# First layer of a graph network: count products taken in pairs between dense steps

## Chip, core and metric

The kernel runs on one core of a Trainium2 chip. The metric is the device time of one execution in microseconds (us). The core has five engines that matter here: TensorE (PE in the profile, and PEld for its weight loads), VectorE (DVE), ScalarE (ACT), GpSimd (POOL), which issues the gathers, and SyncE (SP), which issues plain transfers.

## What is computed

A graph of 6,250 nodes and 100,000 edges, sorted by destination, goes through a layer norm and four layers. Each layer adds up every node's neighbours and passes the sum through three dense stages.

```
def agg(h):
    return jax.ops.segment_sum(h[src], dst, num_segments=N)     # N = 6250
for l in range(3):
    h = x + agg(x)
    h = relu(h @ W1s[l] + b1s[l])
    h = relu(h @ W2s[l] + b2s[l])
    x = h @ W3s[l] + b3s[l]
h = x + agg(x)
...                                   # a last layer of the same form, 256 -> 256 -> 64 -> 256
out = x0 + h                          # x0: the kernel's input; the layers get relu(layernorm(x0))
```

## The kernel before

**Blocks.** The nodes lie in 49 blocks of 128. A part of the destination blocks is summed by gathers: POOL fetches one row per edge (line 1622, `rows<-table,idxN`) and DVE adds them up (line 1658, `sums<-sums,rows`). All other destination blocks, 30 of them in the first layer, are summed by matrix products with a matrix of counts: how many edges lead from node s to node d. The counts are built once, in the first layer, kept in DRAM as bytes (`mat`), and read again in the later layers.

**A dense step.** In `product` (from line 1914) the destination blocks are taken in panels of three or four, and each panel goes over the 49 source blocks. One source block of one panel is a dense step: ACT turns the byte counts into a right operand `a` (line 1908), and PE makes four products with it (line 1937, `agg<-a,XY`: two halves of the channels, each with a rounded value and a remainder), 512 columns wide, or 384 in a panel of three. `a` is made three steps ahead (`AHEAD = 3`), in a ring of five buffers.

**A step that builds counts.** In `build` (from line 1229) one step makes the counts of 16 destination nodes against all source nodes, an eighth of a destination block, with one-hot operands. DVE writes `lo`, 128 x 512 (line 1200, one comparison), for every step, and `hi`, 128 x 784 (line 1200, a comparison and a multiplication), once for two steps. PE then makes four count products with them (line 1254, `bp<-hi,lo`, 98 columns, bf16), and ACT, or DVE in every eighth step, moves the result out of `bp` (lines 1262 and 1264). `lo`, `hi` and the PSUM tile `bp` have two buffers each. The program writes the `lo` of step k+1 at step k, so DVE can be up to two steps ahead of PE, and must wait for the products of step k-1 before it writes `lo` of step k+1. The `hi` of steps k+2 and k+3 follows it.

**Side work.** The generator `listed` (from line 1706) is called once per dense step in the first layer. In seven of its steps DVE prepares short tiles (lines 1817 to 1828, `moved`), PE turns them (line 1835, `bp<-ident,moved`, with a `bp` buffer of the same two), and DVE reads the result into `clT` (lines 1845 to 1847). Below, "the listing" means those seven.

**Order.** All engines' instructions are written out by hand in the order of the Python code, and each engine runs its own in that order. In the first layer the order inside one dense step u is: side work that is due (adds of gathered rows, dense stages of an earlier panel), one step of `listed`, the next `a`, then as many building steps as a table `goals` asks for, then the four products of step u:

```
                prepare(u + 1 + (AHEAD if l == 0 else AHEAD + 2))
                if beside is not None:
                    goal = goals[u - PRE]
                    while built[0] < goal:
                        next(beside)
                        built[0] += 1
```

`goals` is a list with one entry per dense step: the number of building steps that must be done by then. It rises in a straight line over each panel, so that the counts of the next panel are there in time: 28 of 257 are done before the first dense step, and then 28 more in 32 dense steps of the first panel, later 32 in 49, fewer at the end. POOL's gathers are issued by a virtual clock that each product advances by a planned cost (`passed`), and each gather waits for the product that was last written before it.

Of the kernel before, what the change touches and what calls it, by code (L numbers as in the profile page):

```python
# [420 lines left out]
def sorted_edges(  # L421
# [46 lines left out]
    NT = -(-N // P)  # L468
# [628 lines left out]
    with tc.manual_schedule():  # L1097
# [760 lines left out]
        last = [len(panels[l]) - 1 for l in range(NLAYER + 1)]  # L1858
# [99 lines left out]
        def yields(slots):  # L1958
            return UNITS * slots + (slots > TOP)

        total = yields(BUILT)
        built, goals = [0], []
        u0, g0 = 0, UNITS * FIRST + EARLY
        for p in range(last[0] + 1):
# [2 lines left out]
            goals.extend(g0 + (g1 - g0) * (u - u0) // (u1 - u0) for u in range(u0 + 1, u1 + 1))  # L1967
            u0, g0 = u1, g1
        assert g0 == total
        goals = goals + [total] * (NT * (last[0] + 1) - u0)  # L1970
        late = None
        chunks = ctx.enter_context(tc.tile_pool(name="chunks", bufs=1))
        with tc.tile_pool(name="hots", bufs=1) as hots, tc.tile_pool(
# [41 lines left out]
def kernel(  # L2015
# [27 lines left out]
    rest = (x, src, dst, W1s, b1s, W2s, b2s, W3s, b3s, cW1, cb1, cW2, cb2, cW3, cb3, out)  # L2043
    earlier = []
    sorted_edges(tc, good, earlier, *rest)
    done = nc.values_load(good[0:1, 0:1], min_val=0, max_val=1)
    with tc.If(done == 0):
# [27 lines left out]
```

## Time and profile before

| | us |
|---|---|
| median of 3 runs | 2008.25 |
| lowest, highest | 2006.13, 2008.99 |
| profiled execution, its own time | 2005.61 |
| span of its profile | 2003.8 |
| first and last count product | 135.8, 667.4 |
| first dense step | 173.6 |

The profile is of one execution. Its lines give, for a group of equal instructions, the line of the code, the engine, the operation, the tiles written and read (`out<-in`), the count, the busy time, the mean time of one, and the idle time of the engine before them with what ended it. In a timeline each row has the start, the time until the last instruction of the row ends, and in brackets how long the engine had been idle. A PE instruction's time is longer than its share of the pipeline: what matters there is from start to start.

### The profile page before, as it was taken

To read this page: it belongs to the slowest core of one execution; us is meant where nothing else is said; L and a number is where in the kernel's file an instruction comes from. 1 tells how busy PE (TensorE), PEld (TensorE's weight loads), DVE (VectorE), ACT (ScalarE), POOL (GpSimd) and SP (SyncE) were. 2 spreads that over 40 slices of the span, in tenths; PEclk is the share of its full clock that TensorE was granted. 3 is DMA by queue.
4 is the path that set the end of the run, shared out by engine and by line. 5 is a ranking of instruction groups with operands and counts; after the bars stand their busy time and mean duration, and the time that the engine had idled before them with its cause. 6 is when DMAs were issued, how large, how long until landed. Compare 5 with 4: busy or idle time off the path is not lost.

```text
span 2003.8 us, 29049 instructions
## 1 busy us (share of the span) xinstructions
PE 1885.4 (94%) x9236; PEld 1472.8 (74%) x9236; DVE 1034.1 (52%) x2213; ACT 1077.4 (54%) x2164; POOL 1311.1 (65%) x1444
## 2 busy tenths in 40 slices
PE   5955999999999899999999999999999999999997
PEld 3734766777777787777789777777788877777775
DVE  7877887677756343333344353333345354343433
ACT  4734776776766564444445464444445564455442
POOL 2526666766766556777777466676777466777775
PEclk9876999999999999999999999999999999999999
DMA  5523656665656475555656575564657576565553
GB/s 167 176 74 115 201 176 197 203 210 183 206 187 212 155 241 163 173 182 162 185 169 206 168 248 168 159 198 149 187 168 230 160 216 202 184 200 171 180 176 106
DMA packets 252333, 361.40 MB, mean 180 GB/s; under 512 B 33352, under 2 KB 206312, under 8 KB 252154
## 3 DMA queue, kind: packets, MB, share of 16 engines
q1 hardware_dynamic: 188160, 190.34, 30.0%
q0 software_dynamic: 61952, 166.87, 27.5%
q10 hardware_dynamic: 2058, 2.25, 0.4%
q8 instruction: 74, 1.21, 0.3%
q14 instruction: 89, 0.73, 0.1%
HBM read 292.33 MB, written 67.40 MB: 180 GB/s over the span
## 4 chain that ended last, share of the span: by engine, by line
PE 83%; DVE 6%; DMA 4%; issue 2%; POOL 2%; ACT 1%; SPq 0%; DVEq 0%; ACTq 0%; POOLq 0%
PE agg L1937 66%; PE ps L1514 6%; PE ps L1417 6%; DMA rows<-table,idxN 2%; PE bp L1254 2%; POOL rows L1622 1%; DVE hi L1200 1%; PE pt L1685 1%; PE bp L1046 1%; DVE lo L1200 1%; POOL lane L1743 1%; PE ps L1431 1%; DMA wd<-joined,starts 0%; DVE ws L768 0%; DMA lane<-padded,at 0%
## 5 line engine op out<-in xcount | busy, mean ns | idle before, releaser
L1937 PE MATMUL agg<-a,XY 128*128 128x512 f32 (+1 forms) x6272 | 1513.1, 393 | 15.4 <-DVE a L1910 6.9
L1622 POOL DMA_INDIRECT rows<-table,idxN x1121 | 1087.1, 970 | 473.9 <-PE agg L1937 211.0
L1937 PEld LDWEIGHTS agg<-a,XY 128*128 128x128 f32 x6272 | 1146.7, 189 | 249.2 <-issue 12.7
L1908 ACT CAST a<-at 128x512 fp32r<-128x512 uint8 (+1 forms) x1249 | 709.4, 602 | 237.9 <-PE agg L1937 226.8
L1658 DVE TENSOR_TENSOR sums<-sums,rows 128x512 f32<-128x512 f32 x477 | 332.1, 696 | 499.6 <-DMA rows<-table,idxN 444.8
L1910 DVE CAST a<-at 128x512 fp32r<-128x512 uint8 (+1 forms) x312 | 141.7, 460 | 171.4 <-PE agg L1937 147.8
L1262 ACT CAST at<-bp 128x392 uint16<-128x392 f32 x227 | 110.3, 489 | 128.0 <-PE bp L1254 122.2
L1417 PE MATMUL ps<-h,w 128*128 128x512 f32 (+2 forms) x336 | 135.3, 546 | 0.0
L1514 PE MATMUL ps<-w,h 128*128 128x256 f32 x588 | 133.7, 379 | 0.0
L1200 DVE TENSOR_TENSOR lo<-lanes,pairs 128x512 bf16<-128x512 bf16 x256 | 107.1, 424 | 45.1 <-PE bp L1254 44.3
L1254 PEld LDWEIGHTS <-lo 128*128 128x128 bf16 x1028 | 57.5, 103 | 96.8 <-DVE lo L1200 41.9
L1254 PE MATMUL bp<-hi,lo 128*128 128x98 bf16 x1028 | 95.2, 219 | 33.4 <-DVE lo L1200 27.1
L1514 PEld LDWEIGHTS ps<-w,h 128*128 128x128 f32 x588 | 111.2, 190 | 15.9
L596 POOL DMA_INDIRECT table<-zz,ids x72 | 72.9, 1013 | 66.3 <-DVE zz L1519 48.1
L1654 ACT COPY sums<-rows 128x512 f32<-128x512 f32 x74 | 43.8, 593 | 122.5 <-DMA rows<-table,idxN 101.1
L1420 ACT ACTIVATE h<-ps,bias 128x512 f32<-128x512 f32 (+2 forms) x84 | 51.7, 636 | 95.1 <-PE ps L1417 95.1
L1417 PEld LDWEIGHTS ps<-h,w 128*128 128x128 f32 x336 | 63.0, 193 | 52.6 <-issue 37.8
L1519 DVE TENSOR_TENSOR zz<-ps,w 128x512 f32<-128x512 f32 (+1 forms) x81 | 50.5, 639 | 96.0 <-PE ps L1514 89.3
L1693 ACT ACTIVATE h<-pt,bias 128x256 f32<-128x256 f32 (+1 forms) x84 | 33.1, 446 | 124.3 <-PE pt L1685 124.2
L1344 DVE TENSOR_TENSOR XY<-back,XY 128x256 fp32r<-128x256 f32 x138 | 55.1, 423 | 46.9 <-ACT XY L1343 46.0
L1951 ACT ACTIVATE h<-agg,bias 128x512 f32<-128x512 f32 (+1 forms) x60 | 37.6, 671 | 73.3 <-PE agg L1937 73.1
L1200 DVE TENSOR_TENSOR hi<-hi,pairs 128x784 bf16<-128x784 bf16 x128 | 72.6, 568 | 4.4
(235 smaller groups left out, 952.0 us busy)
## 6 DMA issues: line engine op xcount, KB each, us to landing
at<-mat SPq DMA_DIRECT2D x140, 448.0 KB
mat<-at SPq DMA_DIRECT2D x32, 784.0 KB
at<-mat SPq DMA_DIRECT2D x62, 336.0 KB
rows<-table,idxN POOLq DMA_INDIRECT x1121
back<-table SPq DMA_DIRECT2D x138, 128.0 KB
table<-zz SPq DMA_DIRECT2D x35, 256.0 KB
at<-mat SPq DMA_DIRECT2D x63, 112.0 KB
own<-zz SPq DMA_DIRECT2D x55, 128.0 KB
```

What stands on the lines that cost most here:

```text
L596: got = nc.gpsimd.indirect_dma_start(out=ap, out_offset=bass.IndirectOffsetOnAxis(ap=ids[:, b:b + 1], axis=0), in_=sb, in_offset=None)
L1200: nc.vector.tensor_tensor(o, values, which[:, :, None, :].to_broadcast(shape), op)
L1254: mm = nc.tensor.matmul(bp[:, m * HW:(m + 1) * HW], lo[:, m, :], hi[:, m, :], start=(i == 0), stop=(i == len(sets) - 1))
L1262: nc.scalar.copy(o, v)
L1344: later(1, lambda: nc.vector.tensor_tensor(XY[:, j:j + m, C:], z[:, :m, :], XY[:, j:j + m, :C].bitcast(F32), OP.subtract))
L1417: mm = nc.tensor.matmul(ps[:, :w], weights[l][0][:, c, i * P:(i + 1) * P], h1[:, c, :w], start=(c == 0), stop=(c == KC - 1))
L1514: mm = nc.tensor.matmul(o, h2[0][:, c, nodes], w3[:, c, :], start=(c == 0), stop=(c == KC - 1))
L1622: got = nc.gpsimd.indirect_dma_start(out=t[:, c % 2, :], out_offset=None, in_=tables[self.l][:, :], in_offset=bass.IndirectOffsetOnAxis(ap ...
L1658: nc.vector.tensor_tensor(sums, sums, rows.rearrange("p h c -> p (h c)"), OP.add)
L1908: nc.scalar.copy(o, v)
L1910: nc.vector.tensor_copy(o, v)
L1937: mm = nc.tensor.matmul(agg[c][:, :w], XY[:, j, o:o + P], a[:, :w], start=(i == 0 and half == 0), stop=(i == NT - 1 and half == 1))
```

## The change

One line. Each entry of `goals` is rounded up to an even number, but never above the total.

```
         assert g0 == total
-        goals = goals + [total] * (NT * (last[0] + 1) - u0)
+        goals = [min(total, g + g % 2) for g in goals] + [total] * (NT * (last[0] + 1) - u0)
```

So a dense step asks for no building step or for two: the second of each two is taken earlier, right behind the first. No instruction is added or left out. The 229 building steps after the first dense step stand in 228 runs of count products before (once two stand together), and in 115 now.

In the regular stretch, after the listing, the change shows well on ACT. `at<-bp` is one building step that is moved out, `a<-at` one dense step's operand. Before:

```order
L1188 COPY pairs<-clT 128x96
L1262 CAST at<-bp 128x49x8
L1908 CAST a<-at 128x512 x2
L1262 CAST at<-bp 128x49x8
L1908 CAST a<-at 128x512
L1262 CAST at<-bp 128x49x8
```

Now:

```order
L1188 COPY pairs<-clT 128x96
L1262 CAST at<-bp 128x49x8 x2
L1908 CAST a<-at 128x512 x3
L1262 CAST at<-bp 128x49x8 x2
L1908 CAST a<-at 128x512 x3
L1188 COPY pairs<-clT 128x96
```

Where one and two dense steps stood by turns behind a building step, three now stand behind two of them.

In the listing, PE in the difference of the two orders (the rows cut here are the same pairs of a weight load and a count product, four of each to a building step):

```order
 L1254 LDWEIGHTS lo
 L1254 MATMUL bp<-hi,lo 128x98
-L1937 MATMUL agg<-a,XY 128x512 x4
-L1254 LDWEIGHTS lo
-L1254 MATMUL bp<-hi,lo 128x98
...
-L1937 MATMUL agg<-a,XY 128x512 x8
...
+L1937 MATMUL agg<-a,XY 128x512 x12
 L1835 MATMUL bp<-ident,moved 32x32 x8
```

The dense step that stood between two building steps is gone from there, and the pair stands right behind the turn of line 1835: turn, first step, second step use three `bp` tiles in a row, of two buffers.

DVE at the same place. Before, in a row:

```order
L1200 TENSOR_TENSOR lo<-lanes,pairs 128x512
L1845 TENSOR_SCALAR clT<-bp,spot 128x16x2
L1846 CAST clT<-bp 128x16x2
L1847 CAST clT<-spot 128x16x2
L1200 TENSOR_TENSOR lo<-lanes,pairs 128x512
L1200 TENSOR_TENSOR hi<-cols,pairs 128x784
L1200 TENSOR_TENSOR hi<-hi,pairs 128x784
L1817 TENSOR_SCALAR block<-lane 128x31
```

Now:

```order
L1845 TENSOR_SCALAR clT<-bp,spot 128x16x2
L1846 CAST clT<-bp 128x16x2
L1847 CAST clT<-spot 128x16x2
L1200 TENSOR_TENSOR lo<-lanes,pairs 128x512
L1200 TENSOR_TENSOR hi<-cols,pairs 128x784
L1200 TENSOR_TENSOR hi<-hi,pairs 128x784
L1200 TENSOR_TENSOR lo<-lanes,pairs 128x512
L1817 TENSOR_SCALAR block<-lane 128x31
```

The first `lo` here is that of the pair's second step, and it stands behind the three reads of the turn's result, as it did before; the other has moved from in front of those reads to behind the `hi` of the pair before.

On POOL one gather changes its place against a group of scatters, and on SP two loads of counts against a store; all else there is as before.

## Prediction

> **What bounds the kernel now.** I read the page first: how full each engine is, and which chain ended last.
>
> ```profile
> PE 1885.4 (94%) x9236; PEld 1472.8 (74%) x9236; DVE 1034.1 (52%) x2213; ACT 1077.4 (54%) x2164; POOL 1311.1 (65%) x1444
> ...
> PE 83%; DVE 6%; DMA 4%; issue 2%; POOL 2%; ACT 1%; SPq 0%; DVEq 0%; ACTq 0%; POOLq 0%
> ```
>
> PE is the bound of the whole, but the change touches the first layer alone, so I cut that into stages by busy time of each engine (columns: PE, PEld, DVE, ACT, POOL, then the granted clock).
>
> ```profile
> 191.00:236.00 45.00, 40.49 (x284) 34.01 (x283) 40.61 (x106) 33.24 (x80) 29.92 (x30) 0.90 0.57 179
> 236.00:290.00 54.00, 52.13 (x406) 37.15 (x406) 42.61 (x144) 36.45 (x75) 35.42 (x36) 1.00 0.58 183
> 290.00:400.00 110.00, 109.58 (x611) 77.68 (x610) 80.33 (x167) 79.21 (x163) 73.13 (x78) 1.00 0.63 200
> ```
>
> Three stages. From 191 to 236 (panel of three, many building steps) DVE works 40.6 of 45 us, and the rows it adds up keep it waiting for most of the rest:
>
> ```profile
> L1658 DVE TENSOR_TENSOR sums<-sums,rows 128x512 f32<-128x512 f32 x10 | 6.9, 694 | 6.9 <-DMA rows<-table,idxN 6.9
> ```
>
> There DVE is the bound and PE is not. From 236 to 290, with the listing, PE is idle for 1.9 us. From 290 to 667 PE does not stop. So a gain on PE counts from about 237 on, and what goes wrong must come from DVE.
>
> **The gain: fewer switches between count products and dense products.** PE alone in the timeline, in the regular stretch:
>
> ```profile
> 419.14 0.35 PE L1254 MATMUL bp<-hi,lo 128*128 128x98 bf16 x4
> 419.32 2.10 PE L1937 MATMUL agg<-a,XY 128*128 128x512 f32 x8
> 421.26 0.35 PE L1254 MATMUL bp<-hi,lo 128*128 128x98 bf16 x4
> 421.44 1.18 PE L1937 MATMUL agg<-a,XY 128*128 128x512 f32 x4
> 422.46 0.35 PE L1254 MATMUL bp<-hi,lo 128*128 128x98 bf16 x4
> 422.63 2.11 PE L1937 MATMUL agg<-a,XY 128*128 128x512 f32 x8
> 424.58 0.35 PE L1254 MATMUL bp<-hi,lo 128*128 128x98 bf16 x4
> ```
>
> From start to start, a run of four count products and eight dense ones takes 421.26 - 419.14 = 2.12 us, a run and four dense ones 422.46 - 421.26 = 1.20. The difference, 0.92 to 0.93, is one dense step, so a run of four costs 1.20 - 0.93 = 0.27 (2.12 - 1.86 = 0.26 by the other). The one place where two building steps stand together already shows what a run of eight costs:
>
> ```profile
> 477.72 0.52 PE L1254 MATMUL bp<-hi,lo 128*128 128x98 bf16 x8
> 478.06 2.11 PE L1937 MATMUL agg<-a,XY 128*128 128x512 f32 x8
> ```
>
> The first dense product follows the run's start after 0.34 us, where it follows a run of four after 0.18. Four more count products take 0.16 to 0.17, then, and a run of eight 0.43, against 0.52 for two of four: 0.09 us less. The rest of the 0.26 is the switch back. Weight loads, by operand (min/median/max):
>
> ```profile
> L1254 PEld LDWEIGHTS <-lo x1028: 95/99/148, 135.8 to 667.4; 128*128 128x128 bf16 x172
> L1937 PEld LDWEIGHTS agg<-a,XY x6272: 186/188/338, 173.6 to 1986.0; 128*128 128x128 f32 x196
> ```
>
> Behind a dense product of 0.23 us a load of 188 ns hides; behind a count product, whose share is 0.05, it does not, and the first dense step pays for it. A run of eight pays once.
>
> By the order, 190 runs of count products begin after 237 us before, and 96 now: 94 fewer, times 0.09, is 8.5 us. The 19 fewer between 175 and 237 (1.7 us) I count as nothing, since DVE bounds that stage; the ends are 0 and 1.7.
>
> [...]
>
> **What it costs on ACT, POOL and SP.** Two moves out of `bp` follow each other on ACT.
>
> ```profile
> L1908 ACT CAST a<-at 128x512 fp32r<-128x512 uint8 (+1 forms) x1249 | 709.4, 602 | 237.9 <-PE agg L1937 226.8
> L1262 ACT CAST at<-bp 128x392 uint16<-128x392 f32 x227 | 110.3, 489 | 128.0 <-PE bp L1254 122.2
> ```
>
> Two moves are 1.0 us before the next `a`. PE has operands for three dense steps, 2.8 us, and three dense steps follow a pair: hidden. Without that cover the second move, 0.5 us, would be paid at each pair. The pair's two `bp` buffers are free again long before the next pair. Gathers wait for products of PE (the row is in the rivals), keep their order but for one, and come a few tenths of a us apart from where they were: nothing. The two loads of counts on SP are for a panel that starts later: nothing.
>
> **What it costs on DVE: two left operands at once.** Total work there is the same. But the dense step that stood between the two building steps gave DVE 0.93 to 1.86 us to finish the second `lo`; now PE asks for it at once. Two places.
>
> *The listing.* Here the second `lo` stands behind three reads that wait for PE. Before:
>
> ```profile
> 261.79 0.43 PE L1835 MATMUL bp<-ident,moved 128*32 128x32 f32 x16
> 262.14 0.35 PE L1254 MATMUL bp<-hi,lo 128*128 128x98 bf16 x4
> 262.31 0.25 DVE L1845 TENSOR_SCALAR clT<-bp,spot 128x32 bf16<-128x32 f32 x1 [0.80 <-PE bp L1835]
> 262.47 0.18 DVE L1846 CAST clT<-bp 128x32 bf16<-128x32 f32 x1
> 262.57 0.18 DVE L1847 CAST clT<-spot 128x32 bf16<-128x32 f32 x1
> 262.65 0.42 DVE L1200 TENSOR_TENSOR lo<-lanes,pairs 128x512 bf16<-128x512 bf16 x1
> 263.33 0.35 PE L1254 MATMUL bp<-hi,lo 128*128 128x98 bf16 x4
> ```
>
> The first run would be over at 262.14 + 0.17 = 262.31. The second `lo` is there at 262.65 + 0.42 = 263.07, and with a signal's 0.05 the second run starts at 263.12. PE loses 0.8 us, in which a dense step ran before. The third `bp` tile in a row also needs the reads of line 1845 and 1846 done, but that is earlier. The order puts a pair right behind the turn in all seven cases, since building steps come every three dense steps and the listing does too: 7 x 0.8 = 5.6 us. Of that, about 1 us was paid before, as here:
>
> ```profile
> 259.57 0.35 PE L1254 MATMUL bp<-hi,lo 128*128 128x98 bf16 x4 [0.58 <-DVE lo L1200]
> ```
>
> So +4.6 us. The ends: 2.8, if half of it falls into waits that DVE causes there anyway, and 8.8, if a 0.6 us addition of rows is also in front of the `lo` (7 x 1.4 - 1).
>
> *The rest, 290 to 667.* DVE is ahead of PE as a rule and waits for it. What stops it are rows that have not landed:
>
> ```profile
> DVE lo L1200 <- PE bp L1254: 43.9, 48, 3.3
> DVE sums L1658 <- DMA rows<-table,idxN: 22.8, 12, 4.1
> ...
> PE bp L1254 <- DVE lo L1200: 0.6, 1, 0.6
> ```
>
> (237 to 667; total us, times, longest.) Twelve stops, of 1.9 us in the mean, and PE noticed one: the lead of two `lo` and the dense steps between them covered the others. Half of that cover is gone. From below nothing is lost; from above each stop costs one dense step, 12 x 0.93 = 11 us. PE's one wait of 0.6 says the lead was mostly enough, so I stay nearer to the low end: one stop in three, 4 us.
>
> **The sum.** -8.5 + 4.6 + 4.0 = +0.1 us, on the profiled execution's 2005.6 (its span of 2003.8 and 1.8 around it). That execution lies 2.6 us under the median of the three runs, so the forecast there is 2008.4 us: the gain of the switches goes into waits for DVE.
>
> **Rivals.**
>
> *DVE stays ahead* (0.25). The twelve stops stay covered, and the early stage gives its 1.7 us: -8.5 - 1.7 + 4.6 = -5.6, 2002.7 us. For it speaks DVE's own waiting for PE, 43.9 us; against it that the lead is two operands, and a pair uses both.
>
> *The second left operand is late nearly everywhere* (0.33), which makes the kernel slower. In the listing 8.8 us, and at eight or nine of the twelve stops a dense step, 8: -8.5 + 16.8 = +8.3, 2016.5 us. It decides the sign from the point where the waits together pass 12.5 us (8.5 + 4). For it speaks that DVE takes its instructions strictly in turn: at 262.65 the `lo`, whose inputs were old, began only when three reads before it were through; and that adds of rows now stand between the two `lo` of a pair. [...]
>
> *The layer ends with its gathers, not with PE* (within the 0.42 of the forecast). At its end PE waits for the last gathered sums:
>
> ```profile
> 686.58 0.69 PE L1685 MATMUL pt<-ident,u 128*128 128x128 f32 x2 [6.84 <-DVE u L1676]
> ...
> POOL rows L1622 <- PE agg L1937: 46.0, 85, 1.9
> ```
>
> If that end did not follow PE, gain and waits would both vanish in the 6.84 us: 2008 us again. Against it: 85 gathers wait for a dense product, so they move with PE. That the change doesn't do what it says is excluded by the order: 115 runs instead of 228.
>
> **How the numbers follow.** About 0.2%, 4 us, is what a measurement tells from no change. The forecast's own range is 2004 to 2012.4, with 0.42. Faster by more than 4 us has the first rival's 0.25, slower by more the second's 0.33. For 8 in 10 the range reaches down to the first rival with half the listing's cost (-8.5 - 1.7 + 2.8 = -7.4, 2001) and up to the second (2016.5, 2017).
>
> **What would show it.** Right: in the regular stretch runs of eight, three dense steps apart, with 0.43 + 2.79 = 3.22 us from run to run; in the listing four count products, about 0.8 us of idle PE put down to `lo`, four more, seven times; PE's waits for `lo` after 237 grown from 0.6 to about 10 us; the same time from 700 us to the end. Wrong: a run of eight that takes 0.52 (the switch was not the cost), or waits of PE that stay under 3 or pass 16 us, or a wait for `a` behind a pair (ACT, which I priced at nothing).

## Result and profile after

The changed kernel took 2016.95 us in the median of six runs (2016.12 to 2018.09), the kernel before 2008.54 us on the same chip (2006.13 to 2009.06). The ratio is 1.0047, 95% interval 1.0037 to 1.0058: slower by some 9 us. The forecast was 2008.4 us and no change; the time lies above the forecast's own range (2004 to 2012.4), at the upper end of the one for 8 in 10 (2001 to 2017), and at the price of the rival in which the second left operand is late nearly everywhere. The profiled execution took 2016.19 us with a span of 2014.4, 10.6 us more than the one before.

The page of the changed kernel, busy time of each engine and the chain that ended last:

```profile
PE 1878.3 (93%) x9236; PEld 1481.8 (74%) x9236; DVE 1032.9 (51%) x2213; ACT 1072.7 (53%) x2164; POOL 1310.5 (65%) x1444
...
PE 79%; DVE 8%; DMA 6%; issue 3%; POOL 2%; ACT 2%; SPq 0%; DVEq 0%; ACTq 0%; POOLq 0%
```

PE is busy for 7 us less than before; its share of the chain fell from 83 to 79%, and DVE and DMA have more. Busy time by stage (PE, PEld, DVE, ACT, POOL, granted clock, DMA share, GB/s):

```profile
236.00:290.00 54.00, 48.86 (x393) 36.35 (x393) 40.54 (x139) 34.92 (x72) 32.95 (x33) 1.00 0.55 170
290.00:400.00 110.00, 108.52 (x615) 80.78 (x614) 79.56 (x167) 79.02 (x162) 72.41 (x77) 1.00 0.63 197
400.00:500.00 100.00, 96.50 (x546) 73.18 (x545) 68.91 (x147) 65.71 (x137) 62.64 (x64) 0.98 0.60 188
```

In the stage with the listing PE is now idle for 5.1 us, not 1.9. From 290 to 400 it does 615 products where it did 611: there the gain shows. From 400 to 500 it is idle for 3.5 us, and the granted clock is 0.98, not 1.00.

**The gain is there.** PE alone in the regular stretch:

```profile
422.28 0.53 PE L1254 MATMUL bp<-hi,lo 128*128 128x98 bf16 x8
422.63 3.04 PE L1937 MATMUL agg<-a,XY 128*128 128x512 f32 x12
425.51 0.53 PE L1254 MATMUL bp<-hi,lo 128*128 128x98 bf16 x8
425.87 3.04 PE L1937 MATMUL agg<-a,XY 128*128 128x512 f32 x12
428.75 0.53 PE L1254 MATMUL bp<-hi,lo 128*128 128x98 bf16 x8
```

A run of eight and three dense steps take 425.51 - 422.28 = 3.23 us; the prediction said 3.22.

**The waits.** What PE waited for from 237 to 705 us (total us, times, longest):

```profile
PE bp L1254 <- DVE lo L1200: 14.4, 14, 4.3
PE pt L1685 <- DVE u L1676: 5.1, 1, 5.1
PE agg L1937 <- ACT h L1951: 2.4, 7, 0.5
PE bp L1254 <- ACT at L1262: 0.6, 1, 0.6
```

For left operands it is 14.4 us in 14 waits, not 0.6 in one. Seven of the 14 are the listing's, PE and then DVE at one of them:

```profile
267.49 0.43 PE L1835 MATMUL bp<-ident,moved 128*32 128x32 f32 x16
267.85 0.35 PE L1254 MATMUL bp<-hi,lo 128*128 128x98 bf16 x4
268.81 0.35 PE L1254 MATMUL bp<-hi,lo 128*128 128x98 bf16 x4 [0.61 <-DVE lo L1200]
```

```profile
267.99 0.25 DVE L1845 TENSOR_SCALAR clT<-bp,spot 128x32 bf16<-128x32 f32 x1 [0.23 <-PE bp L1835]
268.16 0.18 DVE L1846 CAST clT<-bp 128x32 bf16<-128x32 f32 x1
268.25 0.17 DVE L1847 CAST clT<-spot 128x32 bf16<-128x32 f32 x1
268.34 0.42 DVE L1200 TENSOR_TENSOR lo<-lanes,pairs 128x512 bf16<-128x512 bf16 x1
```

From run to run it is 0.96 us where four more products take 0.17, so 0.79 us are lost, not the 0.61 in the bracket: the first run is shown with 0.35 us, 0.18 more than its share, and that hides 0.18 of the wait.

The two longest waits are elsewhere. At 484 us stands the step that adds up two one-hot sets. PE, then DVE:

```profile
481.17 0.52 PE L1254 MATMUL bp<-hi,lo 128*128 128x98 bf16 x8
483.76 0.38 PE L1254 MATMUL bp<-hi,lo 128*128 128x98 bf16 x4 [2.07 <-DVE lo L1200]
```

```profile
481.73 0.57 DVE L1264 CAST at<-bp 128x392 uint16<-128x392 f32 x1 [1.26 <-PE bp L1254]
482.21 0.56 DVE L1200 TENSOR_TENSOR hi<-cols,pairs 128x784 bf16<-128x784 bf16 x1
482.80 0.57 DVE L1200 TENSOR_TENSOR hi<-hi,pairs 128x784 bf16<-128x784 bf16 x1
483.28 0.75 DVE L1200 TENSOR_TENSOR lo<-lanes,pairs 128x512 bf16<-128x512 bf16 x2
```

Behind that step the code makes `hi` and `lo` of the next one only when its own `bp` is being read. A dense step covered this before; in a pair that straddles the step nothing does. No row of gathers is in it. At 671 us, in the last panel, it is such a row (DVE):

```profile
669.74 0.70 DVE L1658 TENSOR_TENSOR sums<-sums,rows 128x512 f32<-128x512 f32 x1 [3.01 <-DMA rows<-table,idxN]
670.35 0.75 DVE L1200 TENSOR_TENSOR lo<-lanes,pairs 128x512 bf16<-128x512 bf16 x2
```

and PE waits for that second `lo` from 666.6 to 670.8:

```profile
670.82 0.35 PE L1254 MATMUL bp<-hi,lo 128*128 128x98 bf16 x4 [4.26 <-DVE lo L1200]
```

Those rows were late themselves. The gathers stand behind a scatter of a dense stage's result, for which POOL stood still:

```profile
660.42 1.01 POOL L596 DMA_INDIRECT table<-zz,ids  x1 [4.62 <-DMA own<-zz]
```

In the kernel before this scatter came at 650.12, after 2.04 us. PE began the products of that stage 7.4 us later than before (649.81, not 642.39), but DVE the addition that ends it (line 1519) 10.4 us later (654.90, not 644.47), since it stood behind a `lo` that waited 1.50 us for PE and the `hi` that follows. So what DVE waits for holds up the side work behind it. From 237 to 667 us its waits in front of `lo` grew from the 43.9 us that the prediction shows to

```profile
DVE lo L1200 <- PE bp L1254: 78.5, 54, 4.2
```

This chain is read from one trace; no run tests it.

Right behind each of the two long waits of PE, the granted clock fell to a half for 3.4 us (columns as above):

```profile
484.00:487.40 3.40, 3.40 (x11) 2.71 (x9) 2.02 (x5) 1.62 (x3) 1.25 (x2) 0.50 0.72 230
671.70:675.10 3.40, 3.40 (x13) 3.40 (x12) 2.48 (x5) 2.65 (x7) 2.49 (x4) 0.50 0.31 93
```

The 16 dense products behind each wait took 5.37 us (483.93 to 489.30) and 4.44 us (671.00 to 675.44) from start to start, where 3.8 and 2.9 are usual: 1.6 and 1.5 us lost. The kernel before has no such stretch between 217 and 684 us.

**The account**, from 237 us to the second layer's first dense product: all PE's waits went from 10.7 to 22.5 us by their groups, +11.8; 14 of them recorded 0.16 too short (the last count product in front of them is shown with 0.207 us, its share is 0.044), +2.2; half clock, +3.1; 94 pairs at 0.078 us (a run of eight takes 0.446 in the median over its dense neighbours, two of four 0.524), -7.3. The sum is +9.8. By the starts of the same dense products it was 9.3: that one of the second layer came 11.1 us later than before (702.62, not 691.49), of which 0.5 us were there at the very first dense product and 1.3 more at 237 us. From there to the end the difference stays.

### The profile page after: what moved, and what is told of

Read it like the earlier page. It is cut to its first block, busy times and chain, and to the rows that moved or that the text cites. A ratio compares the mean times of both kernels' runs of the same rounds, so it can differ in the third digit from the quotient of the medians.

```text
span 2014.4 us, 29123 instructions
## 1 busy us (share of the span) xinstructions
PE 1878.3 (93%) x9236; PEld 1481.8 (74%) x9236; DVE 1032.9 (51%) x2213; ACT 1072.7 (53%) x2164; POOL 1310.5 (65%) x1444
## 4 chain that ended last, share of the span: by engine, by line
PE 79%; DVE 8%; DMA 6%; issue 3%; POOL 2%; ACT 2%; SPq 0%; DVEq 0%; ACTq 0%; POOLq 0%
PE agg L1937 62%; PE ps L1514 6%; PE ps L1417 6%; DMA rows<-table,idxN 5%; PE bp L1254 2%; DVE lo L1200 1%; DVE hi L1200 1%; PE bp L1046 1%; POOL rows L1622 1%; PE pt L1685 1%; DVE sums L1658 1%; DMA lane<-padded,at 1%; PE ps L1431 1%; DVE ws L768 0%; DVE stats L1003 0%
## 5 line engine op out<-in xcount | busy, mean ns | idle before, releaser
L1937 PE MATMUL agg<-a,XY 128*128 128x512 f32 (+1 forms) x6272 | 1488.9, 392 | 24.5 <-ACT a L1908 10.0
L1908 ACT CAST a<-at 128x512 fp32r<-128x512 uint8 (+1 forms) x1249 | 701.6, 602 | 253.3 <-PE agg L1937 243.7
L1262 ACT CAST at<-bp 128x392 uint16<-128x392 f32 x227 | 104.1, 490 | 102.3 <-PE bp L1254 96.7
L1254 PE MATMUL bp<-hi,lo 128*128 128x98 bf16 x1028 | 80.2, 218 | 44.7 <-DVE lo L1200 43.3
```

Source lines behind the costliest of these rows:

```text
L1254: mm = nc.tensor.matmul(bp[:, m * HW:(m + 1) * HW], lo[:, m, :], hi[:, m, :], start=(i == 0), stop=(i == len(sets) - 1))
L1262: nc.scalar.copy(o, v)
L1908: nc.scalar.copy(o, v)
L1937: mm = nc.tensor.matmul(agg[c][:, :w], XY[:, j, o:o + P], a[:, :w], start=(i == 0 and half == 0), stop=(i == NT - 1 and half == 1))
```

## Experiments

The theory: the pair's gain is real, and is lost where its second left operand is late. The rivals: the operand is late because of the pair's place; the layer's end follows its gathers, so that gain vanishes there. The first four kernels ran together (before: 2006.83 us), so did the next four (2007.06), and the last four (2006.69).

**The place of the pair.** The pair stands where its second step stood, later, not where its first did. The edit does a second thing, too: from the 185th building step on, the pairs count from the next step, so none straddles the step with two one-hot sets:

```
-goals = [min(total, g + g % 2) for g in goals] + ...
+goals = [g - (g + (g >= 185)) % 2 for g in goals] + ...
```

> Pairs as in the change, but the first step of each two waits for the second's place (goals are rounded down, not up). As many runs of eight, so the same gain of 94 x 0.08 = 7.5 us from 237 us on. In the listing a pair now comes one or two dense steps after the turn of line 1835, so DVE has 0.93 us or more for the lo behind the three reads. Theory 1 (the second left operand comes late, by its place): the listing's waits for lo fall from 7 of 0.6 us to under 1 us in all, and the time lies 3 to 7 us under the change's: 2010 to 2014. Rival (a pair is dear wherever it stands): 2017 again, within 2 us.

Measured: 2009.0 us, ratio 1.0013 (1.0004 to 1.0023). PE's waits from 237 to 705 us:

```profile
PE bp L1254 <- DVE lo L1200: 10.2, 7, 3.8
PE pt L1685 <- DVE u L1676: 5.2, 1, 5.2
```

This kernel takes 7 us less than the changed one, but the place of the pairs doesn't explain it. In the listing the waits did not fall to under 1 us, as expected: five of the seven stand there, 5.1 us, the longest (2.7) behind rows for which DVE had stopped for 4.66 us, others because the second `lo` now stands behind the preparation of the next turn (lines 1817 to 1828). By the starts of the same dense products this kernel lost 4.4 us from 237 to 290 us, the changed one 2.4. From 290 to 639 us it gained 5.2, where the changed one lost 3.5, and 3.3 of those lie at the step with two sets. The kernel with that second edit alone comes below, at 1.0017: beside it the later place shows no gain.

At 648 us this kernel was 3.5 us ahead of the one before, but 1.9 of these were there at its first dense product; then came a wait of 3.77 for `lo` in the last panel, and at the layer's end it was level within 1 us.

**All pairs but the listing's, and those alone.** The listing lies in the entries 60 to 81 of `goals`:

```
+goals = [g if 60 <= i < 82 else min(total, g + g % 2) for i, g in enumerate(goals)] + ...   # without
+goals = [min(total, g + g % 2) if 60 <= i < 82 else g for i, g in enumerate(goals)] + ...   # alone
```

> Pairs everywhere but in dense steps 60 to 81, the listing, which keep the table of before. Theory 1: the listing's 3 us go away, with some seven pairs' gain (0.6 us) lost: 2013 to 2014.5. Rival (the loss is spread over all pairs): 7 of 113 pairs less, 0.6 us: 2016.4.

> The table of before, with pairs in dense steps 60 to 81 alone, the listing. Theory 1: seven waits of 0.6 us for lo, some 0.8 from start to start, less 0.6 of gain: 3 us slower than before, 2011 to 2012.5. Rival (spread over all pairs): within 0.7 us of before, 2008.5 to 2009.5.

Measured: without the listing 2012.92 us, 1.0028 (1.0016 to 1.0039); the listing alone 2010.99, 1.0022 (1.0010 to 1.0033). The listing costs 0.0019 to 0.0022, 4 us; the rest, 0.0028, is 5.6 us, so pairs lose also where DVE has time enough in the mean. The kernel without the listing has both long waits, 2.07 us at 481 and 4.38 at 668.

**Left operands further ahead.** Four `lo` buffers, each written two building steps ahead (one buffer of gathered rows fewer, for the room):

```
-lo = hots.tile([P, BATCH, P], BF16, name="lo", bufs=2)
+lo = hots.tile([P, BATCH, P], BF16, name="lo", bufs=4)
...
-low_hot(hots, k + 1)
+low_hot(hots, k + 2)
```

> The change, with lo in four buffers instead of two and written two building steps ahead, so that both operands of a pair can be ready before it begins; the room comes from the ring of gathered rows (eight buffers instead of nine). Theory 1: PE's waits for lo after 237 us fall from 14 us to under 4 (the turn's bp buffer and rows that land late are left), the clock no longer drops at 484 and 672 us, and the gain of the switches shows: 2001 to 2006, faster than before. Rival (runs of eight are themselves slow, or the gathers' order costs it): 2014 or more.

Measured: 2007.94 us, 1.0004 (0.9995 to 1.0014). PE's waits (two lines more stand above some, three above others, so 1254 is 1256 and 1685 is 1688):

```profile
PE pt L1688 <- DVE u L1679: 10.2, 1, 10.2
PE bp L1256 <- ACT at L1264: 2.4, 4, 0.6
PE bp L1838 <- DVE moved L1831: 2.2, 1, 2.2
PE bp L1256 <- DVE lo L1200: 2.1, 1, 2.1
```

The loss in the time is gone, but the gain that was expected (2001 to 2006) did not come. The wait for `lo` fell from 14.4 to 2.1 us, the one at the step with two sets. Behind the listing this shows the theory's first half: from 290 to 668 us this kernel gained 4.3 us on the one before by the starts of the same dense products, where the changed one lost 8.8. In the listing it lost 4.5 us all the same, to waits for `moved` and for the moves out of `bp`. And the wait at the layer's end rose to 10.2. What sets that end? POOL at the end of the first layer, in the kernel before:

```profile
678.65 0.95 POOL L1622 DMA_INDIRECT rows<-table,idxN  x1 [0.30 <-issue]
679.91 0.95 POOL L1622 DMA_INDIRECT rows<-table,idxN  x1 [0.30 <-issue]
681.16 0.95 POOL L1622 DMA_INDIRECT rows<-table,idxN  x1 [0.30 <-issue]
682.42 0.95 POOL L1622 DMA_INDIRECT rows<-table,ids  x1 [0.30 <-issue]
```

Gather follows gather every 1.25 us, and the profile shows nothing else that POOL waits for. With the operands ahead it is the same to the last one:

```profile
683.46 0.94 POOL L1625 DMA_INDIRECT rows<-table,idxN  x1 [0.30 <-issue]
684.71 0.95 POOL L1625 DMA_INDIRECT rows<-table,ids  x1 [0.30 <-issue]
```

Then come the rows, the sums and `u`: PE goes on 4.2 us behind the last gather in both, at 686.6 and at 688.9. The prediction held against this that 85 gathers wait for a dense product. They do, earlier on; the last ones don't.

**Gathers sooner in the first layer.** The pace at which rows are asked for is planned so that the last is due 2 us before the layer's planned end; here 12, on four bases: before, pairs later, operands ahead, changed.

```
-self.pace = (begun[self.l] + work_of(self.l) - CLOSE - self.first) / len(self.order)
+self.pace = (begun[self.l] + work_of(self.l) - CLOSE - (10.0 if self.l == 0 else 0.0) - self.first) / len(self.order)
```

> The kernel before, with one number changed: the gathers of the first layer are paced so that the last is due 12 us before the layer's planned end, not 2. In the kernel before PE waits 6.84 us at 686.6 us for the last gathered sums, and POOL asks for gathers and scatters one right behind another from 650 us on. Theory 'the first layer ends with its gathers': the last gather comes some 8 to 10 us sooner, the wait falls to 1 to 2 us, and the time falls by about 5 us, to 2002 beside 2007. Rival 'the gathers are only late because PE is': they wait for dense products and move with them; the wait stays at 5 to 7 us and the time within 1 us. Second rival: gathers asked for sooner stop DVE elsewhere, waits of PE for lo in 290 to 667 grow by several us, and the time stays or rises.

> Pairs taken at the place of their second building step (from the 185th on), and the gathers of the first layer due 10 us sooner. With the pairs alone this kernel was 3.5 us ahead of the one before at 648 us and level with it at the layer's end. Theory 'the layer ends with its gathers': those 3.5 us come out, and the time is 2 to 4 us under that of the kernel before with the same pacing, about 2000. Rival 'second left operand late': the late operands in the last panel (3.77 us at 659) eat the lead again, and the time is level with that of the kernel before with the same pacing, or 1 to 2 us over it.

> The changed kernel with the left operands written two building steps ahead (four buffers), and the gathers of the first layer due 10 us sooner. With the first alone PE's waits for lo were 2.7 us, not 19, and the wait at the layer's end grew to 10.2 us. Theory 'the gain of the pairs is there and hidden by the gathers': the wait at the end falls to 1 to 3 us and the time to 1998 to 2001, 2 to 5 us under the kernel before with the same pacing. Rival 'a pair saves nothing worth speaking of': level with the kernel before with the same pacing, 2002.

> The changed kernel, with the gathers of the first layer due 10 us sooner, and nothing else. Here the pair's second left operand is as late as in the changed kernel: seven waits in the listing and the others, 19 us in all. Theory 'the late operand and the gathers are two separate losses': the time falls by about 5 us from 2017, to 2011 to 2013, and stays 8 to 10 us over the kernel before with the same pacing. Rival 'the late operands of the last panel were the gathers' doing': the wait of 4.26 us at 671 goes too, with the half-clock stretch behind it, and the time falls by 10 us or more, to 2005 to 2007.

| base | alone | with sooner gathers | wait at the first layer's end |
|---|---|---|---|
| before | 1 | 1.0006 (0.9997 to 1.0015) | 6.8 to 3.1 us |
| pairs later | 1.0013 | 1.0035 (1.0022 to 1.0047) | 5.2 to 2.5 |
| operands ahead | 1.0004 | 0.9998 (0.9990 to 1.0007) | 10.2 to 2.1 |
| changed | 1.0047 | 1.0041 (1.0027 to 1.0055) | 5.1 to 2.0 |

The waits fell as the theory has it, the times did not: none of the four came out at the number expected. In the changed kernel the wait of 4.26 us in the last panel went as well (the longest for `lo` is 2.1 now), and the time still fell by 1 us only. With pairs later, sooner rows also made PE wait 11.6 us for `lo`, not 10.2. And what was won at that end was lost at the next layer's. Waits of PE from 705 to 1200 us in the first of the four, where the kernel before has 2.9:

```profile
PE pt L1685 <- DVE u L1672: 7.0, 1, 7.0
```

In the other three it is 6.8, 7.3 and 7.8. The second layer's end waits for its own gathers, which were not asked for sooner.

**Gathers sooner in all layers, the operands, and pairs in good places.** `CLOSE` goes from 2 to 12 for all layers: alone, with operands ahead, and with operands ahead and pairs. Pairs stand outside the listing only, and behind the step with two one-hot sets (`odd`) they count from the next step, so that none straddles it. A fourth kernel is the changed one with that last edit alone:

```
+odd = UNITS * (TOP + 1)
+goals = [min(total, g + (g + (g > odd)) % 2) for g in goals] + ...
```

> The changed kernel, with the pairs counted anew behind the building step that adds two one-hot sets, so that none straddles it (there PE waited 2.07 us at 484 us for the second left operand, and the granted clock then stood at half for 3.4 us). Theory 'the long stop and the half clock behind it cost 2.1 + 1.7 us': both are gone, and the time is 3 to 4 us under that of the changed kernel, about 1.003 of the kernel before. Rival 'the half clock is not the stop's doing': a half-clock stretch stays near 484, and the time falls by 2. Second rival 'the gathers set the layer's end': the lead is there at 500 us and gone at 700, with a longer wait for u, ratio 1.0047 as before.

> The kernel before, with the gathers of every layer due 10 us sooner. With the first layer's alone the wait at its end fell from 6.8 to 3.1 us, but the second layer's end wait for gathered sums grew from 2.9 to 7.0. Theory 'the gathers set the end of each layer': that wait falls too, and the time is 2 to 5 us under the kernel before. Rival 'POOL cannot ask sooner': the waits stay, and so does the time, within 1 us.

> The kernel before with the gathers of every layer due 10 us sooner and the left operands two building steps ahead, single steps: the control of the run above. Both theories: within 1 us of the kernel with the sooner gathers alone, since PE waits for lo only 0.6 us there. Rival 'the lead itself gains or costs': 2 us or more off it.

> Pairs outside the listing only, none that straddles the step with two one-hot sets, left operands two building steps ahead, gathers of every layer due 10 us sooner. Some 80 pairs after 290 us at 0.078 us are 6 us. Theory 'a pair gains 0.08 us where its second operand is ready and nothing else sets the end': 4 to 6 us under the same kernel with single steps (the next run). Rival 'the pair's gain does not exist': level with it. Second rival 'new waits come in its place': 0 to 2 us under it, with those waits to be seen on PE.

| kernel | median us | ratio |
|---|---|---|
| changed, no pair astride the step | 2010.31 | 1.0017 (1.0008 to 1.0025) |
| before, gathers sooner | 1997.28 | 0.9948 (0.9933 to 0.9962) |
| the same, operands ahead | 1996.27 | 0.9946 (0.9932 to 0.9961) |
| the same, pairs in good places | 1992.59 | 0.9923 (0.9908 to 0.9939) |

The same four kernels had run once before, while the kernel before took 2183.78 us, and in the traces of two of the four PE waited up to 2.5 and 3.5 us for nothing that the profile shows: ratios 1.0051, 0.9954, 0.9980 and 0.9952, in this order, with intervals of 0.004 about them, which tell nothing of a few us.

The first: 6 us of the changed kernel's 9 are gone, more than the 3 to 4 expected. PE at the place now:

```profile
481.55 0.35 PE L1254 MATMUL bp<-hi,lo 128*128 128x98 bf16 x4 [0.58 <-DVE lo L1200]
```

No half clock follows (1.00 from 478 to 490 us); measured from the first dense product, 3.1 us of the gain are there at 488 us. Another 4.4 came from there to the layer's end, half of it in the last panel, where the pairs now lie otherwise and the longest wait is 1.7 us, not 4.3. The parts can't be told apart in the time, only in the trace.

The second: the gathers do bear on the ends of the layers. Due 10 us sooner in all four, they give 9.4 us, more than the 2 to 5 expected, in a kernel with single steps, and the 7.0 in the second layer is gone. In its trace PE's waits for `u` in all layers fall from 12.9 to 7.9 us, and the time behind PE's last product from 9.9 to 7.5; the rest of the 9.4 is not taken apart. The operands' lead, with its one buffer of rows fewer, gives nothing alone (0.9946 against 0.9948). With both covers in place the pairs give 1996.27 - 1992.59 = 3.7 us, a little under the 4 to 6 expected, and this kernel beats both others. PE there, and the control with single steps:

```profile
419.52 0.53 PE L1256 MATMUL bp<-hi,lo 128*128 128x98 bf16 x8
419.88 3.04 PE L1940 MATMUL agg<-a,XY 128*128 128x512 f32 x12
422.76 0.53 PE L1256 MATMUL bp<-hi,lo 128*128 128x98 bf16 x8
```

```profile
419.02 0.35 PE L1256 MATMUL bp<-hi,lo 128*128 128x98 bf16 x4
419.19 2.10 PE L1940 MATMUL agg<-a,XY 128*128 128x512 f32 x8
421.14 0.35 PE L1256 MATMUL bp<-hi,lo 128*128 128x98 bf16 x4
421.31 1.18 PE L1940 MATMUL agg<-a,XY 128*128 128x512 f32 x4
422.33 0.35 PE L1256 MATMUL bp<-hi,lo 128*128 128x98 bf16 x4
```

Two single steps and three dense ones take 422.33 - 419.02 = 3.31 us, a pair and three dense ones 3.24. From the 400th dense product to the 800th the control takes 132.8 us and the kernel with pairs 130.4, with 32 pairs: 0.075 each.

## Why the prediction was wrong in its sum, and right in parts

**The gain.** Right in kind, a little large: 0.075 to 0.078 us a pair, not 0.09, 7.3 us, not 8.5. The runs of eight, three dense steps apart, came as forecast. The switch back is there in both traces: from 290 to 667 us, from the first dense product behind count products to the next it is 0.317 us in the median, where 0.23 is usual between two dense products.

**The early stage, at nothing.** Wrong: from the first dense product to 237 us the changed kernel lost 1.3 us, and PE's waits for `lo` from 173 to 237 us rose from 1.9 to 4.6. The two other kernels with the same pairs there lost 1.6 and 1.7 in that stretch, the one with pairs in the listing alone 0.2. The prediction took a gain on PE as hidden where DVE is the bound (40.6 of 45 us busy from 191 to 236), but PE and DVE can still hold each other up more than before; which of the two did it here is not taken apart. Of the 6.9 us for which rows kept DVE waiting, 5.5 lie before 191 us, too.

**ACT, POOL, SP at nothing.** Right for ACT: one wait of 0.56 us for `at`, none for `a` behind a pair. Wrong for POOL's gathers, though not in the changed kernel's sign: at the layer's end they are a bound of their own.

**The listing, +4.6.** Right: seven waits, each 0.79 us by the starts (one 1.1), where 0.8 was said, and 4 us by two experiments, each with an interval of some 2 us to either side.

**The rest, +4.** This is the step that failed. The prediction priced a stop at one dense step and took one stop in three. PE's seven waits for `lo` outside the listing are 14.4 - 4.65 = 9.8 us by the record, 1.1 more by the starts, and 3.1 for the half clock behind two of them: 14 us, past the upper end of 11. Two prices were wrong. A stop costs what it lasts: with both operands of a pair spent, the whole 4.26 us were PE's. And the 2.07 at 484 were not among the twelve stops at all; the prediction quoted that very run of eight (477.72, two one-hot sets) as the sample for the gain, and did not ask who makes the next operand behind it. The half clock was not foreseen, either.

**The rivals.** "The second left operand is late nearly everywhere" gave the time, 2016.5, but not by its mechanism: PE's waits outside the listing are seven, not eight or nine of twelve row stops, and two of them hold two thirds; that its number fits is luck. "The layer ends with its gathers" was weighed as a case of no change, and the changed kernel did not follow it, since its last gather came 11.2 us later as well (693.58, not 682.42); POOL was 10.2 of these behind at 664 us, after the late scatter. It is one reason why the mended kernels gained nothing until the gathers were paced anew; the listing is the other.

**What would show it.** The waits for `lo` grew to 14.4, within the 16 that I named as the limit, but not to 10; the same time from 700 us on was right.

## What to carry to other kernels

Work that is taken in larger lots needs its operands ahead by a whole lot: count the buffers and, at each place where the producer's order is not the regular one, ask who makes the second operand. A stop in front of the bound engine can cost its whole length, and more behind it: here 4.26 us, and 1.5 at half clock. Before a saving on the bound engine is counted, ask for each stage what else ends it, and look at the last few instructions there, not at the mean: a queue that mostly waits for the bound engine can be the bound at the end, as POOL's was here, where PE went on 4.2 us behind the last gather.

## What the hardware showed

The clock fell after some stops of 2 us. In the profiled executions of the kernel before and the changed one, after 237 us, PE stopped three times for 2.0 to 2.5 us, and two of these stops (2.09 us before, 2.07 in the changed kernel) were followed by 3.4 us at half the clock, the third (2.05, changed) was not. Of three stops of 2.5 to 3.5 us one had 3.4 us behind it (2.76, changed), two had none (2.92 and 2.96). With all three longer ones (4.26, 5.06, 6.84) came a stretch of 3.4 to 6.8 us that began during the stop or behind it. Two stops of 1.8 us in the kernel before had 3.4 us behind them, too, and a third had none, so 2 us is no limit here. With the operands ahead a stop of 2.07 us at the step with two sets had no slower pace behind it (16 dense products in 484.34 - 480.53 = 3.81 us); with sooner gathers besides, 12 behind the same stop are shown with 4.44 us, where 3.04 is usual. What decides it after a stop of 2 us stays open.

In the same two traces POOL gives out a gather every 1.25 us at best, 0.95 of work and 0.30 between two; so 16 gathers that are left at a layer's end take 20 us, an estimate from the two.
